# Selective scan: repeated matmuls into the same PSUM place, and stand-in pieces in the first image

## The chip, the cores and the metric

One core of one Trainium2 chip. The metric is the device time of the whole program in microseconds. The kernel before took 27451.21 us, the median of three runs (27438.02 to 27468.17). A difference is told against that kernel, run on the same chip.

## The reference

The input is eight images of 64 x 64 positions with 96 channels, in float32. Four layers follow one another, each as `x = x + layer(group_norm(x))`:

- Layers 0 and 2 are selective scans over four orders of the positions (rows, columns, and both backwards). With 192 inner channels, 16 states for each and `L = 4096` positions, the core of it is

```python
def step(h, inp):
    ut, dt, bt, ct = inp
    dA = jnp.exp(dt[..., None] * A4)
    dBu = (dt * ut)[..., None] * bt[:, :, None, :]
    h = h * dA + dBu
    y = jnp.einsum('bkdn,bkn->bkd', h, ct)
    return (h, y)
```

  around which stand a projection in, a 3 x 3 convolution per channel, a norm, a gate and a projection out.
- Layer 1 is a scan in chunks with one decay per head, made of matmuls.
- Layer 3 doubles the resolution by a low-pass filter along both axes (matmuls with fixed 64 x 128 matrices), applies `h @ W1.T`, a quadratic polynomial and `h @ W2.T`, and filters down again.

## The kernel before

The images are worked one after the other. Layers 0 to 2 of an image run in order; layer 3 of an image, called the slow layer here, is cut into small pieces that run *beside* the two selective scans of the next image (`slow_layer`, lines 433 to 627; `Beside`, 629 to 688). Layer 3 of the last image runs by itself at the end (`spectral_layer`).

`selective_scan` (lines 690 to 1034) is what the change touches. It goes through 32 steps: for each of four orders k, eight chunks of 512 positions. A step has six units n of 32 channels with 4 of the 16 states on 128 partitions, four groups of states side by side, so that a tile is 128 x 2048. For a unit:

- PE spreads `du` (32 channels) over 128 partitions into the PSUM tile `pu` by one matmul with a 0/1 matrix of 32 rows (`spread`, L835).
- DVE multiplies `pu` by `b` (`with_b`, L841); for two units of six POOL does it, from another copy `du2`.
- ACT makes the decays `da` in PSUM (L856), and DVE scans, two groups at a time (`scan`, L871).
- ACT copies the last state (L887), then POOL multiplies `h` by `c` in place (L892).
- PE sums `h` over the states, for three units at once, in `total_y`: one matmul that adds the direct term (L899), then twelve with 128 rows and 32 columns (L909). ACT copies the result out (L1008, L1016).

Beside that, `prepare` works ahead for the step after next: two projections on PE (L742, L752) that ACT copies out (L747, L756), softplus, and DMAs that copy `b`, `c`, `dx` and `du` to all partitions. For k = 1 and 3 the image is read by columns, through a view of 64 x 8 elements at a stride (`view`, L421).

All the order is written by hand (`tc.manual_schedule`, lines 977 to 1032): every engine takes its instructions in the order in which this loop writes them. On PE a step reads: spread of unit 1, `total_y` of the step before, spread of unit 3, up to three pieces, spread of unit 4, `total_y`, one piece, L742, sometimes a fifth piece, spread of the next step's unit 0, L752. `pu` has one PSUM buffer, under the tag `misc`, which pieces four and five share; the pieces before it, `pv` and `py` share one under the tag `py`. So a spread waits until DVE has read the `pu` before it, and a piece until ACT has copied out what stood in the buffer.

A piece is a tuple: a load, an ACT preparation, the PE part, the ACT copy of its result, a store, and how far ahead to load. `Beside.begin` runs the PE part (`op[2](ps)`), `Beside.end` the copy (`op[3](ps)`). There are 139 entries for the first scan of an image and 137 for the third layer's scan; `quota` gives a step four of them, now and then five. In the column pieces (`cols`, seven for each of 32 columns): one that filters along the height (L499), three hidden layers (L516, squared by ACT at L523), two mixes (L532, L536; copied out at L547) and one that filters down (L555). The first image has no slow layer beside it, and its lists are empty.

Of the kernel before, what the change touches and what calls it, by code (L numbers as in the profile page):

```python
# [53 lines left out]
K_TF = K_GRP + 96  # L54
# [13 lines left out]
def tile_vision_stack(  # L68
# [19 lines left out]
    nc = tc.nc  # L88
# [4 lines left out]
    def resident(name, src, shape):  # L93
        t = wp.tile(shape, F32, name=name)
        nc.sync.dma_start(t, src)
        return t

    cst = resident("cst", consts[:, :K_TF], [128, K_TF])
# [9 lines left out]
    sel = cst[:DM, K_SEL:K_RED]  # L108
    red = cst[:, K_RED:K_ID]
    ident = cst[:, K_ID : K_ID + 128]  # L110
# [38 lines left out]
    with (  # L149
# [6 lines left out]
        for i, (dtw, dtx, w) in enumerate(((dt0, dx0, w0), (dt2, dx2, w2))):  # L156
# [12 lines left out]
            for k in range(K):  # L169
                pw = pp.tile([DM, 2, 192], F32, name="pw", bufs=2)  # L170
                for hf in range(2):
# [4 lines left out]
                        start=True,  # L176
                        stop=True,
# [255 lines left out]
    def slow_layer(prev):  # L433
# [3 lines left out]
        pool = [None]  # L437
# [8 lines left out]
        def rows(j):  # L446

            def load():
                if j % 2 == 0:
                    live["xs", j] = xs = wide("sx")[:DM]  # L450
                    nc.sync.dma_start(xs, xd[:, j * 256 : j * 256 + 512])

            def norm():
                if j % 2 == 0:
                    live["xn"] = xn = wide("sn")[:DM]
                    nc.scalar.activation(
                        xn, live["xs", j], AF.Identity, scale=sb[:, 0:1], bias=sb[:, 1:2]
                    )

            def turn(ps):  # L460
                pt = ps[:64, : 4 * DM].rearrange("p (i c) -> p i c", i=4)
                for i in range(4):
                    at = (j % 2) * 256 + 64 * i
                    nc.tensor.transpose(pt[:, i, :], live["xn"][:, at : at + 64], ident[:DM, :DM])

            def turned(ps):
                live["xt"] = xt = narrow("st", "g")
                nc.scalar.copy(xt[:64].rearrange("p i c -> p (i c)"), ps[:64, : 4 * DM])

            def across(ps):  # L470
                nc.tensor.matmul(
                    ps[:, : 4 * DM],
                    up,
                    live["xt"][:64].rearrange("p i c -> p (i c)"),
                    start=True,
                    stop=True,
                )

            def crossed(ps):
                live["x1"] = x1 = wide("sw")[:, : 4 * DM]  # L480
                nc.scalar.copy(x1, ps[:, : 4 * DM])

            def store():
                nc.sync.dma_start(
                    x1d[4 * j : 4 * j + 4].rearrange("h w c -> w h c"),
                    live["x1"].rearrange("p (h c) -> p h c", h=4),
                )

            return [(load, norm, turn, turned, None, 4), (None, None, across, crossed, store, 0)]

        def cols(n):

            def load():
                live["c1"] = c1 = narrow("sc", "x1")[:64]
                nc.sync.dma_start(c1, x1d[:, 4 * n : 4 * n + 4])

            def down_h(ps):
                for i in range(4):
                    nc.tensor.matmul(  # L499
                        ps[:DM, i * 128 : i * 128 + 128],  # L500
                        live["c1"][:, i, :],
                        up,
                        start=True,
                        stop=True,
                    )

            def fine(ps):
                live["x2"] = x2 = wide("s2")[:DM]
                nc.scalar.copy(x2, ps[:DM])
                live["f"] = []  # L510

            ops = [(load, None, down_h, fine, None, 4 if n else 0)]
            for m in range(3):

                def hidden(ps, m=m):
                    nc.tensor.matmul(  # L516
                        ps, w3as[:, m * 128 : (m + 1) * 128], live["x2"], start=True, stop=True
                    )

                def square(ps, m=m):  # L520
                    f = wide("sf")
                    live["f"].append(f)
                    nc.scalar.activation(f, ps, AF.Square, bias=b1q[:, m : m + 1])  # L523

                ops.append((None, None, hidden, square, None, 0))
            for p in range(2):

                def mix(ps, p=p):
                    for i in range(2):
                        at = (2 * p + i) * 128  # L530
                        po = ps[:, i * DM : i * DM + DM]
                        nc.tensor.matmul(  # L532
                            po, live["x2"][:, at : at + 128], w12, start=True, stop=False
                        )
                        for m in range(3):
                            nc.tensor.matmul(  # L536
                                po,
                                live["f"][m][:, at : at + 128],
                                w2q[:, m, :],
                                start=False,  # L540
                                stop=(m == 2),
                            )

                def mixed(ps, p=p):
                    if p == 0:
                        live["g"] = narrow("sg", "g")
                    nc.scalar.copy(  # L547
                        live["g"][:, 2 * p : 2 * p + 2, :].rearrange("p i c -> p (i c)"),
                        ps[:, : 2 * DM],
                    )  # L550

                ops.append((None, None, mix, mixed, None, 0))

            def lower(ps):
                nc.tensor.matmul(  # L555
                    ps[:64, : 4 * DM],
                    down,
                    live["g"].rearrange("p i c -> p (i c)"),
                    start=True,
                    stop=True,  # L560
                )

            def lowered(ps):
                nc.scalar.copy(
                    live["g"][:64].rearrange("p i c -> p (i c)"), ps[:64, : 4 * DM]
                )

            def store():
                nc.sync.dma_start(
                    g2d[4 * n : 4 * n + 4].rearrange("w h c -> h w c"), live["g"][:64]  # L570
                )

            ops.append((None, None, lower, lowered, store, 0))
            return ops

        def ends(j):
# [39 lines left out]
                    live["res"].rearrange("p (h c) -> p h c", h=4),  # L616
                )

            return [(load, shift, last, done, store, 1 if j else 0)]

        def flat(parts):
            return [op for part in parts for op in part]
# [2 lines left out]
        first = flat(rows(j) for j in range(16)) + gap + flat(cols(n) for n in range(SPLIT))  # L625
        second = flat(cols(n) for n in range(SPLIT, 32)) + gap + flat(ends(j) for j in range(16))
        return pool, (first, second)

    class Beside:

# [29 lines left out]
        def begin(self, pool, tag):  # L660
            if self.at >= len(self.ops):
                return
            op = self.ops[self.at]
            if op:
                ps = pool.tile([128, LC], F32, name="ps", tag=tag)
                op[2](ps)
                self.flush()
                self.open = (op, ps)
            else:
                self.flush()  # L670
                self.open = (None, None)

        def end(self):
            if not self.open:
                return
            op, ps = self.open
            self.open = None
            if op:
                op[3](ps)
                self.waiting = op[4]  # L680
            self.at += 1
            if self.loaded <= self.at < len(self.ops):
                self.flush()
                while self.loaded <= self.at:
                    self.load(self.loaded)
            self.prepare(self.at)
            self.ahead(self.at)


    def selective_scan(w, wdt, a, d, u, y, beside):  # L690
# [23 lines left out]
        with (  # L714
# [11 lines left out]
            pool, ops = beside  # L726
# [100 lines left out]
                nc.scalar.copy(places(db, NSG, int(k >= 2)), src)  # L827
                made[i]["db", n] = db

            def spread(t):  # L830

                m, n = made[t // units], t % units
                rows = slice(32 * (n % 3), 32 * (n % 3) + 32)
                m["pu"] = pu = pmp.tile([128, LC], F32, name="pu", tag="misc")
                nc.tensor.matmul(pu, sel[rows, :], m["du"][rows, n // 3, :], start=True, stop=True)  # L835

            def with_b(t):

# [125 lines left out]
            with tc.tile_pool(name="p_da", bufs=1, space=PSUM) as pap:  # L964
# [4 lines left out]
                states = {}  # L969
                for t in range(3):  # L970
                    enter(t)
                spread(0)
                decays(0, 0)
                decays(0, 1)
                with_b(0)
# [1 line left out]
                for t in range(total + 2):  # L977
                    n, i = t % units, t // units
# [4 lines left out]
                    elif n == 5 and quota > 4:  # L983
                        other.begin(pmp, "misc")
                    if n in (0, 3, 5) and ahead:
                        spread(t + 1)
                    elif n == 1 and t + 2 < total:
                        spread(t + 2)
                    if n == 0 and i > 0:
                        sums = total_y(i - 1, 1)  # L990
                    elif n == 3:
# [573 lines left out]
    prev = None  # L1565
    for b in range(batch):
        xd = xp.tile([DM, L], F32, name="xd")
        sb3 = sb3s[b % 2]
        pool, ops = slow_layer(prev) if prev else ([None], ((), ()))
        layers = (  # L1570
            (w0s, w0, lambda u, y: selective_scan(w0s, wdts[0], a0s, dsum[0], u, y, (pool, ops[0]))),
            (w1s, w1, lambda u, y: chunked_scan(w1s, w1, dsum[1], u, y)),
# [47 lines left out]
        prev = (xd, sb3, dst)  # L1620
# [151 lines left out]
```

## Time and profile before

| | |
|---|---|
| profiled execution | 27478.66 us |
| its span, first to last instruction | 27476.7 us |
| mean granted TensorE clock | 0.763 |
| PE busy | 23020.0 us, 91061 matmul instructions |
| DVE busy | 24006.6 us |
| POOL busy | 21792.7 us |
| ACT busy | 16531.6 us |
| DVE scans L871 | 6144 of 2282 ns |
| POOL products L892 | 3072 of 4174 ns |
| spreads L835 | 4096 instructions (two for each float32 matmul) of 904 ns |
| scans of the first image, first to last L871 | 1185.0 and 1184.6 us |
| the 14 later ones | 1223.1 to 1241.1 us |

A group in the profile reads: line, engine, operation, out<-in with its shapes, how often; then busy time, mean ns of one, and the idle time of the engine just before, with what ended it. In a line of a timeline the start and the duration stand first. A float32 matmul stands as two MATMUL instructions. A busy PE is not PE at its peak, since the granted clock changes the duration of the same instruction; PEclk shows it, as a share of full speed.

### The profile page before, as it was taken

What the parts mean: (1) busy time and instruction counts of PE and PEld (TensorE: products, weight loads), DVE (VectorE), ACT (ScalarE), POOL (GpSimd) and SP (SyncE); (2) the same over time, 40 slices, a digit from 0 to 9 for tenths busy, and PEclk for the clock granted to TensorE, in tenths of its full rate; (3) what the DMA queues carried; (4) which work ended last, traced back from release to release, by engine and by line L of the source; (5) the groups of instructions that cost most, each with busy time, mean ns of one, the idle gap of its engine ahead of it and who ended that gap; (6) DMA issues with size and microseconds to landing.
All of it is one profiled execution on the core that took longest, in us unless ns stands there. A gap on an engine that the chain in (4) does not pass through costs nothing. (4 is left out here: it accounts for less than half of the span.)

```text
span 27476.7 us, 283336 instructions
## 1 busy us (share of the span) xinstructions
PE 23020.0 (84%) x91061; PEld 8527.1 (31%) x91061; DVE 24006.6 (87%) x17105; ACT 16531.6 (60%) x29953; POOL 21792.7 (79%) x8360
## 2 busy tenths in 40 slices
PE   7787788888888888888888888888888888888888
PEld 2141222422224222242223422234222342223424
DVE  8979898798988989889898898988989889898896
ACT  5646565565655656556565565655656556565564
POOL 8949798597976979769797697976979769796694
PEclk7787777877778777787777877778777787777878
DMA  4415454154531545325453254532545325453252
GB/s 120 119 33 126 111 131 104 43 129 115 134 99 48 129 115 134 93 54 129 115 130 89 57 129 116 130 86 61 128 117 132 80 68 127 117 131 75 71 129 67
DMA packets 1681706, 2831.73 MB, mean 103 GB/s; under 512 B 434984, under 2 KB 478280, under 8 KB 1675616
## 3 DMA queue, kind: packets, MB, share of 16 engines
q1 hardware_dynamic: 1663584, 2807.32, 41.8%
q8 instruction: 730, 11.96, 0.2%
q10 hardware_dynamic: 16640, 6.29, 0.1%
q14 instruction: 752, 6.16, 0.1%
HBM read 2385.11 MB, written 427.49 MB: 102 GB/s over the span
## 5 line engine op out<-in xcount | busy, mean ns | idle before, releaser
L871 DVE TENSOR_TENSOR_SCAN h<-da,db 128x1026 f32<-128x1026 f32 x6144 | 13775.7, 2282 | 751.3 <-ACT da L856 446.0
L892 POOL TENSOR_TENSOR h<-h,c 128x2048 f32<-128x2048 f32 x3072 | 12774.4, 4174 | 1129.8 <-ACT state L887 571.0
L909 PE MATMUL py<-h,cst 128*32 128x512 f32 x24576 | 5331.0, 788 | 105.4 <-POOL h L892 105.0
L841 DVE TENSOR_TENSOR db<-pu,b 128x2048 f32<-128x2048 f32 x2048 | 4652.1, 2272 | 625.5 <-PE pu L835 616.7
L856 ACT ACTIVATE da<-dx,a2s 128x512 f32<-128x512 f32 x6144 | 4239.2, 690 | 1536.9 <-DVE h L871 1390.5
L856 ACT ACTIVATE da<-dx,a0s 128x512 f32<-128x512 f32 x6144 | 4239.5, 690 | 1527.6 <-DVE h L871 1379.6
L841 POOL TENSOR_TENSOR db<-du,b 128x2048 f32<-128x2048 f32 x1024 | 4649.7, 4541 | 569.6 <-ACT db L827 569.6
L835 PE MATMUL pu<-du,cst 32*128 32x512 f32 x4096 | 3328.7, 904 | 1203.6 <-DVE db L841 1070.1
L909 PEld LDWEIGHTS py<-h,cst 128*32 128x32 f32 x24576 | 1207.3, 140 | 4828.1 <-issue 4366.2
L742 PE MATMUL pv<-u,wk 96*96 96x512 f32 x2048 | 1502.1, 864 | 556.6 <-ACT y L1016 444.4
L835 PEld LDWEIGHTS pu<-du,cst 32*128 32x128 f32 x4096 | 811.4, 246 | 3234.7 <-DVE db L841 1612.8
L752 PE MATMUL pv<-u,wk 96*128 96x512 f32 x2048 | 1590.7, 911 | 54.3 <-ACT raw L747 53.3
L899 PE MATMUL py<-y,cst 96*96 96x512 f32 x1536 | 1506.6, 1078 | 6.4 <-ACT state L887 6.4
L516 PE MATMUL ps<-s,w3as 96*128 96x512 f32 x1344 | 998.0, 833 | 544.8 <-ACT sf L523 188.1
L1285 ACT ACTIVATE sg<-sg 128x768 f32<-128x768 f32 x1024 | 820.5, 801 | 838.1 <-PE sg L1269 838.1
L887 ACT COPY state<-h 128x4 f32<-128x4 f32 x3072 | 591.9, 193 | 864.4 <-DVE h L871 862.5
L1239 POOL TENSOR_TENSOR ce<-ec,cr 112x512 f32<-112x512 f32 x256 | 529.0, 2066 | 717.3 <-ACT ec L1237 699.0
L1317 DVE TENSOR_TENSOR wt<-wt,cbm 128x768 f32<-128x768 f32 x1024 | 991.4, 1003 | 117.0 <-ACT wt L1286 116.3
L536 PE MATMUL ps<-w3bs,sf 128*128 128x96 f32 x5376 | 1043.9, 349 | 0.0
L1216 POOL TENSOR_TENSOR rr<-lr,cc 128x768 f32<-128x768 f32 x256 | 376.5, 1471 | 758.5 <-ACT lr L1214 753.4
L319 POOL TENSOR_SCALAR xn<-xs,sb 96x512 f32<-96x512 f32 x192 | 203.3, 1060 | 972.3 <-PE pz L324 486.2
L536 PEld LDWEIGHTS ps<-w3bs,sf 128*128 128x128 f32 x5376 | 964.6, 263 | 0.0
(241 smaller groups left out, 30528.9 us busy)
## 6 DMA issues: line engine op xcount, KB each, us to landing
dx<-dd SPq DMA_DIRECT2D x4096, 192.0 KB
b<-bcd SPq DMA_DIRECT2D x2048, 256.0 KB
c<-bcd SPq DMA_DIRECT2D x2048, 256.0 KB
du<-dud SPq DMA_DIRECT2D x2048, 128.0 KB
dd<-raw SPq DMA_DIRECT2D x1024, 192.0 KB
dud<-du SPq DMA_DIRECT2D x512, 128.0 KB
xd<-xs SPq DMA_DIRECT2D x256, 192.0 KB
cr<-bcd SPq DMA_DIRECT2D x1536, 32.0 KB
```

The lines of the kernel that those rows point to most:

```text
L516: nc.tensor.matmul(ps, w3as[:, m * 128 : (m + 1) * 128], live["x2"], start=True, stop=True)
L536: nc.tensor.matmul(po, live["f"][m][:, at : at + 128], w2q[:, m, :], start=False, stop=(m == 2),)
L742: nc.tensor.matmul(pv[:DM], weights[k][:, hi, 128:], uv[hi], start=(hi == 0), stop=(hi == 1))
L752: nc.tensor.matmul(pv, weights[k][:, hi, :128], uv[hi], start=(hi == 0), stop=(hi == 1))
L835: nc.tensor.matmul(pu, sel[rows, :], m["du"][rows, n // 3, :], start=True, stop=True)
L841: (nc.gpsimd if pool else nc.vector).tensor_mul(groups(m["db", n]), (m["du2"][:, n // 3, :] if pool else m["pu"]) .unsqueeze(1) .to_broadc ...
L856: nc.scalar.activation(dst[:, g, :LC], made[i]["dx"][n // 3][:, n % 3, :], AF.Exp, scale=av4[:, k, n, gs : gs + 1],)
L871: nc.vector.tensor_tensor_scan(made[i]["h", n][:, at][:, way], das[p][:, rev : 2 * SEG + rev][:, way], made[i]["db", n][:, at][:, way], 0. ...
L892: nc.gpsimd.tensor_mul(h, h, made[i]["c"])
L899: nc.tensor.matmul(py, skip[:, hf, :] if k == 0 else ident[:DM, :DM], view((u if k == 0 else y)[:, hf, :], wh, c * LC, LC), start=True, st ...
L909: nc.tensor.matmul(py[32 * q : 32 * q + 32, :], red, hs[q][:, g, :], start=False, stop=(g == NSG - 1),)
L1317: nc.vector.tensor_mul(it["wt"], it["wt"], m["cbm"][:, j : j + 1, :].to_broadcast([128, RK, Q]),)
```

## The change

The number of times that PE makes the same result is written into the loop. Each copy starts anew at the same place (`start=True`), so the result does not change.

- `spread` gets a count. The spreads of units 0 and 1 are made twice, that of unit 3 three times, that of unit 4 once; the very first once.
- Every piece gets a seventh entry, the count: two for all but the mixes, which keep one. `Beside.begin` runs the PE part that often.
- In the first image, where the lists were empty, 138 stand-in pieces are put beside each of the two scans: a matmul of the identity (128 rows) with 384 columns of constants, made twice, whose result nobody reads or copies.

Nothing changes on DVE, POOL or the DMA queues; ACT's work is the same.

```diff
-            return [(load, norm, turn, turned, None, 4), (None, None, across, crossed, store, 0)]
+            return [(load, norm, turn, turned, None, 4, 2), (None, None, across, crossed, store, 0, 2)]
...
-            ops = [(load, None, down_h, fine, None, 4 if n else 0)]
+            ops = [(load, None, down_h, fine, None, 4 if n else 0, 2)]
...
-                ops.append((None, None, hidden, square, None, 0))
+                ops.append((None, None, hidden, square, None, 0, 2))
...
-                ops.append((None, None, mix, mixed, None, 0))
+                ops.append((None, None, mix, mixed, None, 0, 1))
...
-            ops.append((None, None, lower, lowered, store, 0))
+            ops.append((None, None, lower, lowered, store, 0, 2))
...
-            return [(load, shift, last, done, store, 1 if j else 0)]
+            return [(load, shift, last, done, store, 1 if j else 0, 2)]
...
+    def busy(ps):
+        nc.tensor.matmul(ps[:, :K_TF], ident, cst, start=True, stop=True)
+
+    idle = [(None, None, busy, None, None, 0, 2)] * 138
...
                 ps = pool.tile([128, LC], F32, name="ps", tag=tag)
-                op[2](ps)
+                for _ in range(op[6]):
+                    op[2](ps)
...
-                op[3](ps)
+                if op[3]:
+                    op[3](ps)
...
-            def spread(t):
+            def spread(t, times):
...
-                nc.tensor.matmul(pu, sel[rows, :], m["du"][rows, n // 3, :], start=True, stop=True)
+                for _ in range(times):
+                    nc.tensor.matmul(
+                        pu, sel[rows, :], m["du"][rows, n // 3, :], start=True, stop=True
+                    )
...
-                        spread(t + 1)
+                        spread(t + 1, 1 if n == 3 else 2)
                     elif n == 1 and t + 2 < total:
-                        spread(t + 2)
+                        spread(t + 2, 3)
...
-        pool, ops = slow_layer(prev) if prev else ([None], ((), ()))
+        pool, ops = slow_layer(prev) if prev else ([None], (idle, idle))
```

## The prediction

> **What bounds the kernel.** I read the page first, then who waited for whom on DVE, then two steps of a scan in order of time, then the granted clock in stretches of 1 us. A "step" is one 512-column chunk, six units; a scan has 32 steps, and 16 scans make 512 steps.
>
> ```profile
> PE 23020.0 (84%) x91061; PEld 8527.1 (31%) x91061; DVE 24006.6 (87%) x17105; ACT 16531.6 (60%) x29953; POOL 21792.7 (79%) x8360
> L841 DVE TENSOR_TENSOR db<-pu,b 128x2048 f32<-128x2048 f32 x2048 | 4652.1, 2272 | 625.5 <-PE pu L835 616.7
> L835 PE MATMUL pu<-du,cst 32*128 32x512 f32 x4096 | 3328.7, 904 | 1203.6 <-DVE db L841 1070.1
> ```
>
> No engine is full over the span, but in a scan DVE and POOL nearly are. A step has 12 scans of 2.24 us and four products of 2.27 us on DVE: 36.0 us. POOL has six products of 4.17, two of 4.54 and du: about 36.5. So a step can hardly be under 36.25 us (a step's length is the distance between the same instruction in two steps: L835 at 234.56 and 270.81 in the trace). PE waits for DVE 1070 us at L835, so it has room. The question is when its results come. DVE's waits, largest first:
>
> ```profile
> DVE db L841 <- PE pu L835: 616.7, 388, 5.5
> DVE h L871 <- ACT da L856: 446.0, 606, 8.4
> ```
>
> Nearly all of the 617 us stands at one place. Sorted by place in the step, 538 us is the product of the *next step's unit 0*. It is unlike in two kinds of steps. In scans k = 1 and 3 the image is read turned (64x8 elements at a stride), in k = 0 and 2 plainly. A turned step of the first image:
>
> ```profile
> 600.52 3.65 PE L742 MATMUL pv<-u,wk 96*96 96x512 f32 x4 [1.80 <-ACT state L887]
> 604.11 2.01 PE L835 MATMUL pu<-du,cst 32*128 32x512 f32 x2
> 606.15 2.29 DVE L841 TENSOR_TENSOR db<-pu,b 128x2048 f32<-128x2048 f32 x1 [1.55 <-PE pu L835]
> 609.76 2.07 PE L835 MATMUL pu<-du,cst 32*128 32x512 f32 x2
> 612.95 2.27 DVE L841 TENSOR_TENSOR db<-pu,b 128x2048 f32<-128x2048 f32 x1
> ```
>
> L742 takes 3.65 us, the spread behind it 2 us, and DVE loses 1.55. This step takes 38.07 us (609.76 to 647.83). A plain step:
>
> ```profile
> 264.03 1.96 PE L742 MATMUL pv<-u,wk 96*96 96x512 f32 x4 [2.27 <-ACT y L1016]
> 265.92 1.12 PE L835 MATMUL pu<-du,cst 32*128 32x512 f32 x2
> 268.49 2.27 DVE L841 TENSOR_TENSOR db<-pu,b 128x2048 f32<-128x2048 f32 x1
> ```
>
> Here L742 takes half as long, the spread too, and it is ready 1.45 us before DVE takes it. Why does the spread cost 2.07 us in one and 1.12 in the other? The clock (the last three columns are PEclk, DMA share, GB/s):
>
> ```profile
> 602.00:603.00 1.00, 1.00 (x2) 0.18 (x1) 1.00 (x2) 0.00 (x0) 1.00 (x2) 1.00 0.47 160
> 604.00:605.00 1.00, 1.00 (x2) 0.44 (x2) 0.60 (x1) 0.74 (x2) 1.00 (x1) 0.60 0.65 193
> 606.00:607.00 1.00, 1.00 (x2) 0.50 (x2) 0.85 (x1) 0.97 (x5) 1.00 (x2) 0.50 0.00 0
> 611.00:612.00 1.00, 1.00 (x2) 0.24 (x2) 1.00 (x1) 0.97 (x2) 1.00 (x2) 0.50 0.26 66
> ```
>
> PE is busy in every one of these microseconds, yet the clock falls from 1 to 0.5 at 604.2 and stays there until 617.8, in the middle of L909.
>
> **What holds the clock: rule against rows.** The change keeps PE busier. The Trainium skill (TensorE: Matmul & The Clock Gate, Part 1) says that the gate watches how busy PE is in free-running windows of about 3.4 us: one busy window releases full clock, an idle one takes it away. The trace agrees on the grid (the clock changes only at multiples of 3.413 us) but not on "busy". I compared each window with the clock of the next. At half clock, windows full of L258 or L337 (96 rows, plain) mostly raise it, 0.7 of a window of L909 (128 rows) does; where spreads (32 rows) fill 0.4 to 0.6 of a window and other matmuls as much (0.4 to 0.6), none of 460 or so raised it. At full clock a window is held by about half a window of 96-row work; a spread's time counts there about 0.4 of that. Full windows of turned L742 kept the clock in 0 of 36, since it reads at half the rate (1.03 us an instruction against 0.59 for plain). So I take work as rows times columns moved, not time busy. By the page's rule the added copies hold the full clock everywhere (first rival below). By the rows they can't in a turned step: from L742 (3.65 us) over the spread, turned L752 and the next spread, some ten us hold nothing that counts as half, so the clock falls there as it does now.
>
> **The change, part by part.** *One more copy* of a spread is two instructions, 1.71 us at half clock, 0.86 at full (their spacing in L909: 0.86 and 0.43). DVE waits for the last copy. Per step four spreads become eight: 6.9 us of PE at half clock, 3.4 at full. PE is busy 26 us of a first-image step, 32.7 of 38.6 later, so it fits as a sum; what counts is each place.
>
> 1. Turned steps, unit 0 (twice): the copy is straight on DVE's path. Now 24 of 32 such steps in the first image and 183 of 224 later wait there. 30 and 41% of these spreads begin at full clock, fewer would end so, and I take the copy at full in a quarter: 0.25 x 0.86 + 0.75 x 1.71 = 1.50 us. 207 x 1.50 = 310, and half of it for the other 49 steps: 37. **+347.**
> 2. Turned steps, unit 1 (twice): it comes behind L752 at half clock; ready at 611.83, taken at 612.95, 1.12 spare. 1.71 - 1.12 = 0.59 in 256 steps. **+151.**
> 3. Plain steps, unit 0: 1.45 us spare hides a copy at full clock (0.86); if that cover is gone it costs 0.9 to 1.7. The 112 steps of 256 that wait already pay 1.28, the middle of both clocks. **+143.** Unit 1 has 2.7 spare: nothing.
> 4. Unit 3 (three times): 7 us between it and DVE's use cover it, as does a half-clock copy. Unit 4 stays single: nothing. But pieces queue behind the triple.
> 5. Pieces beside (first layer 139, third 137; 4 a step and a fifth in 20 steps an image): a doubled L516 takes 1.98 us at full clock, 2.07 single at half, so where the clock is held a copy is free. The fifth stands between L742 and the spread: 5 of 7 column pieces are doubled, 0.93 us on average in 140 steps, 130, of which plain steps cover some. **+100.** The other pieces: ACT copies each out in order, and POOL's product waits behind ACT (POOL h on ACT state, 571 us now). Bounds: nothing, if they run at full clock (59 to 70% begin so now), and 1.7 us a step and more if not. I take nothing, as most begin at full.
> 6. Stand-ins in the first image: 128 rows x 384, two copies, 1.28 us at full clock, 2.56 at half; no copy-out, no DMA. Three fit into the 9.7 us that PE waits before unit 4's spread. They hold the clock there but not up to L742. Between -57 (64 steps from 37.14 to 36.25) and +60: I take nothing.
> 7. Relief: where the clock now holds longer, totals L909 and the unmultiplied mixes (L536) come sooner. DVE waits 80 us after unit 3 and 150 before unit 5's second scan in later images; half of it. **-115.**
>
> Sum: 347 + 151 + 143 + 100 - 115 = +626 us. The profiled execution took 27478.7 us (span 27476.7); with it 28105, and the median of runs stands 0.1% below: **28080**.
>
> **Rivals.** *The clock holds* (faster). If busy time is what counts, or if pieces and triples bridge the gaps of the plain steps, all copies run at 0.86. Turned steps keep their 1.5 us (L742 stays 3.65, doubled spread 1.98 against 2.07: 256 x 1.5 = 384 of the 617 us stays), and of the 446 us on ACT 0.34 a step stays, as in the shortest steps. 233 + 270 at most, some 400 likely: 27050. For it: the stand-ins and L516 count fully. Against: 604.2. It decides at L742: full clock over that spread in most steps means this. Chance 0.16. *Half clock takes the pieces too* (slower still): after the triple spread (2.6 us that count 0.4) PE idles until y is copied, the clock falls, three doubled pieces cost 1.2 us more each at half clock, ACT and POOL wait behind them: about 2 us more in 448 steps, 28950. For it: totals that run sooner leave longer gaps. Against: L909 now ends so late at half clock that the next window is safe. 0.21. *It all falls into PE's idle time* (no difference), since PE waits for DVE 1070 us: 27450 within 55; against it speaks the 1.55 us above. 0.06. The likeliest: 0.57, 27700 to 28450.
>
> Range: down into the first rival, up to the centre of the second, 27300 to 28950; left out is about 0.11 below and 0.08 above. Faster by over 0.2% (what a measurement can tell from no change) 0.17, within 0.05, slower 0.78.
>
> **What would show it.** Turned steps: unit 0's spread at 3.7 us rather than 2.07, DVE's wait there near 3 us, the wait for PE over all from 617 to some 1200 us; unit 1 in turned steps waiting about 0.6; steps of the first image near 40 where they were 38.07, plain ones at 36.3 to 37. I am wrong if PEclk in the scans rises from 0.72 to 0.85 or more while DVE's wait for PE shrinks, or if ACT's waits for pieces (L547 674 us, L523) double.

## The result, and the profile after

The changed kernel takes 28576.85 us (median of 4 runs, 28567.69 to 28611.54) against 27458.74 before on the same chips: ratio 1.0411, 95% interval [1.0393, 1.0429], +1118 us. The forecast was +626 us, 28080, in a range of 27300 to 28950.

Lines move by 7 to 10: L835 is now L843, L841 is L851, L742 and L752 are L749 and L759, L871 is L881, L909 is L919. From the page of the changed kernel, its totals and the groups that answer to those shown:

```profile
PE 25737.0 (90%) x101605; PEld 9970.3 (35%) x101605; DVE 24063.2 (84%) x17105; ACT 16541.4 (58%) x29953; POOL 21772.0 (76%) x8360
L851 DVE TENSOR_TENSOR db<-pu,b 128x2048 f32<-128x2048 f32 x2048 | 4662.8, 2277 | 1343.6 <-PE pu L843 1322.2
L843 PE MATMUL pu<-du,cst 32*128 32x512 f32 x8160 | 5165.0, 761 | 443.3 <-DVE db L851 324.7
```

DVE, ACT and POOL do the same work in nearly the same time; PE has 10544 instructions more. One spread instruction became faster (761 ns against 904), because the mean clock rose from 0.763 to 0.816. Yet DVE waits for spreads 1322 us where it was 617. DVE's waits in the changed kernel:

```profile
DVE db L851 <- PE pu L843: 1322.2, 791, 7.5
DVE h L881 <- ACT da L866: 649.6, 558, 9.0
```

The second line, 446 before, says that ACT too is late with the decays. Two of the things that it waits for (ACT's waits, changed kernel; L763 copies out L759, L523 a piece):

```profile
ACT raw L763 <- PE pv L759: 1219.3, 385, 5.1
ACT sf L523 <- PE ps L516: 954.3, 630, 2.8
```

The same two waits in the kernel before:

```profile
ACT raw L756 <- PE pv L752: 781.5, 380, 3.9
ACT sf L523 <- PE ps L516: 189.3, 308, 1.1
```

A turned step of the first image, in order of time:

```profile
552.88 3.65 PE L749 MATMUL pv<-u,wk 96*96 96x512 f32 x4 [3.20 <-ACT state L897]
556.46 3.77 PE L843 MATMUL pu<-du,cst 32*128 32x512 f32 x4
560.16 3.78 PE L759 MATMUL pv<-u,wk 96*128 96x512 f32 x4
560.27 2.29 DVE L851 TENSOR_TENSOR db<-pu,b 128x2048 f32<-128x2048 f32 x1 [3.32 <-PE pu L843]
563.88 3.78 PE L843 MATMUL pu<-du,cst 32*128 32x512 f32 x4
567.69 2.29 DVE L851 TENSOR_TENSOR db<-pu,b 128x2048 f32<-128x2048 f32 x1 [0.55 <-PE pu L843]
```

Unit 0's doubled spread takes 3.77 us where one took 2.01, and DVE waits 3.32 us where it was 1.55. Unit 1's comes 0.55 late, where it had been early. The clock over this stretch (third column from the end):

```profile
552.00:553.00 1.00, 0.12 (x1) 0.12 (x2) 1.00 (x2) 1.00 (x4) 1.00 (x1) 1.00 0.42 94
553.00:554.00 1.00, 1.00 (x2) 0.34 (x3) 1.00 (x1) 0.97 (x2) 1.00 (x1) 0.67 0.03 8
555.00:556.00 1.00, 1.00 (x2) 0.00 (x0) 1.00 (x1) 0.00 (x0) 1.00 (x2) 0.50 0.32 107
559.00:560.00 1.00, 1.00 (x2) 0.00 (x0) 0.00 (x0) 0.97 (x2) 1.00 (x2) 0.50 0.00 0
```

It falls within L749, at 553.4, and stays at half through both doubled spreads, until 573.8, though PE is busy all the time in each of the last three stretches shown. By kind of step, from the distance between scans: in the first image plain steps went from 36.60 to 39.34 us and turned ones from 37.71 to 40.64; later from 37.89 to 39.59 and from 39.49 to 41.85. The share of time at full clock went up in all four, later from 0.46 to 0.60 and from 0.40 to 0.57. So the clock did rise, and the steps became longer.

### The profile page after: what moved, and what is told of

Read it like the earlier page. It is cut to its first block, busy times and chain, and to the rows that moved or that the text cites. A ratio compares the mean times of both kernels' runs of the same rounds, so it can differ in the third digit from the quotient of the medians.

```text
span 28609.8 us, 304424 instructions
## 1 busy us (share of the span) xinstructions
PE 25737.0 (90%) x101605; PEld 9970.3 (35%) x101605; DVE 24063.2 (84%) x17105; ACT 16541.4 (58%) x29953; POOL 21772.0 (76%) x8360
## 5 line engine op out<-in xcount | busy, mean ns | idle before, releaser
L881 DVE TENSOR_TENSOR_SCAN h<-da,db 128x1026 f32<-128x1026 f32 x6144 | 13782.7, 2283 | 1062.1 <-ACT da L866 649.6
L851 DVE TENSOR_TENSOR db<-pu,b 128x2048 f32<-128x2048 f32 x2048 | 4662.8, 2277 | 1343.6 <-PE pu L843 1322.2
L843 PE MATMUL pu<-du,cst 32*128 32x512 f32 x8160 | 5165.0, 761 | 443.3 <-DVE db L851 324.7
L919 PE MATMUL py<-h,cst 128*32 128x512 f32 x24576 | 4972.4, 738 | 169.4 <-POOL h L902 168.6
L851 POOL TENSOR_TENSOR db<-du,b 128x2048 f32<-128x2048 f32 x1024 | 4646.2, 4537 | 569.2 <-ACT db L834 569.2
L843 PEld LDWEIGHTS pu<-du,cst 32*128 32x128 f32 x8160 | 1652.0, 224 | 3680.9 <-issue 2749.4
L919 PEld LDWEIGHTS py<-h,cst 128*32 128x32 f32 x24576 | 1149.1, 132 | 4479.1 <-issue 3613.6
L749 PE MATMUL pv<-u,wk 96*96 96x512 f32 x2048 | 1496.7, 861 | 421.7 <-ACT y L1026 291.7
L516 PE MATMUL ps<-s,w3as 96*128 96x512 f32 x2688 | 1605.9, 727 | 245.1 <-ACT sf L523 163.2
L759 PE MATMUL pv<-u,wk 96*128 96x512 f32 x2048 | 1610.3, 921 | 52.0 <-ACT raw L754 52.0
L909 PE MATMUL py<-y,cst 96*96 96x512 f32 x1536 | 1385.1, 993 | 1.6 <-ACT state L897 1.5
L523 ACT ACTIVATE sf<-ps,w3bs 128x512 f32<-128x512 f32 x672 | 461.2, 686 | 954.3 <-PE ps L516 954.3
L763 ACT COPY raw<-pv 128x512 f32<-128x512 f32 x512 | 298.7, 583 | 1220.6 <-PE pv L759 1219.3
L516 PEld LDWEIGHTS ps<-s,w3as 96*128 96x128 f32 x2688 | 531.7, 218 | 1184.5 <-issue 505.8
```

Of the source, the lines that this page charges most:

```text
L516: nc.tensor.matmul(ps, w3as[:, m * 128 : (m + 1) * 128], live["x2"], start=True, stop=True)
L749: nc.tensor.matmul(pv[:DM], weights[k][:, hi, 128:], uv[hi], start=(hi == 0), stop=(hi == 1))
L759: nc.tensor.matmul(pv, weights[k][:, hi, :128], uv[hi], start=(hi == 0), stop=(hi == 1))
L851: (nc.gpsimd if pool else nc.vector).tensor_mul(groups(m["db", n]), (m["du2"][:, n // 3, :] if pool else m["pu"]) .unsqueeze(1) .to_broadc ...
L881: nc.vector.tensor_tensor_scan(made[i]["h", n][:, at][:, way], das[p][:, rev : 2 * SEG + rev][:, way], made[i]["db", n][:, at][:, way], 0. ...
L909: nc.tensor.matmul(py, skip[:, hf, :] if k == 0 else ident[:DM, :DM], view((u if k == 0 else y)[:, hf, :], wh, c * LC, LC), start=True, st ...
```

## The experiments

Theory 1 is that a copy costs where another engine waits for it, and that 32-row copies don't hold the clock. Theory 2 is that the doubled pieces, through ACT, are the main cause. Theory 3 is that PE simply has too much work.

### One part at a time

**Spreads alone**: pieces once, no stand-ins.

```diff
-                for _ in range(op[6]):
+                for _ in range(1):
...
-        pool, ops = slow_layer(prev) if prev else ([None], (idle, idle))
+        pool, ops = slow_layer(prev) if prev else ([None], ((), ()))
```

> The changed kernel with every piece made once and no stand-ins: only the spreads are repeated (2, 2, 3, 1). Theory 1 (a copy costs where DVE waits for it, at half clock; 32-row copies do not hold the clock): the spreads carry more than half of the +1118 us, 28050 to 28250 us; unit 0's wait of DVE (after n5) rises from 538 to 900 or more. Theory 2 (the doubled pieces hold ACT, and POOL and DVE behind it): the spreads alone cost under 300 us, below 27760. Theory 3 (PE has too much work, wherever it stands): the cost goes by added instructions, 4064 of 10544, so 430 us, 27890.

28410.75 us, ratio 1.0343 [1.0326, 1.0361], +934: more than theory 1 gave, far above the others. DVE's wait after unit 5 is 1056 us (538 before). The run's clock, and DVE's wait for spreads over all:

```profile
core 0: 28393.9 us, clock 0.761
```

```profile
DVE db L851 <- PE pu L843: 1363.7, 784, 7.1
```

4064 more PE instructions and PE busy for 89% of the span where it was 84%, and yet the clock stays at 0.761 (0.763 before). The 32-row copies did not raise it.

**Pieces and stand-ins alone**: every spread once.

```diff
-                        spread(t + 1, 1 if n == 3 else 2)
+                        spread(t + 1, 1)
...
-                        spread(t + 2, 3)
+                        spread(t + 2, 1)
```

> The changed kernel with every spread made once: pieces doubled as in the change, stand-ins in the first image. Theory 1: a doubled piece at full clock takes as long as a single one at half clock, so 100 to 450 us above before, 27560 to 27900. Theory 2: 700 us or more, above 28160. Theory 3: 6480 of 10544 added instructions, about 690 us, 28150. If the pieces (96 and 128 rows) hold the clock and nothing else is late, it is below 27400.

28010.43 us, ratio 1.0201 [1.0184, 1.0219], +533, clock 0.795. Above theory 1's range and below the others': the pieces cost more than I had allowed, but they are not the larger part.

**Unit 0 once**, the rest of the change kept.

```diff
-                        spread(t + 1, 1 if n == 3 else 2)
+                        spread(t + 1, 2 if n == 0 else 1)
```

> The changed kernel, but unit 0's spread is made once (unit 1 twice, unit 3 three times, pieces doubled). Theory 1: DVE's wait after unit 5 goes back from 972 us to about 540, and unit 1 is on time in turned steps again (-100): 500 us below the changed kernel, 28000 to 28150. Theory 2: within 150 us of the changed kernel, 28430 to 28580. Theory 3: 1024 fewer instructions of 10544, -110 us, 28470.

28248.31 us, ratio to before 1.0281 [1.0266, 1.0297], +771. That is 347 less than the +1118 of the whole change, so a little above theory 1's range and far from the other two. DVE's wait after unit 5 came back to 510 us as theory 1 says, but not all of that reached the end: the waits after unit 3 and at unit 5's second scan stayed, 292 and 320 us in later images (80 and 150 before). Nor was unit 1 on time again: it still waits 141 us (158 in the changed kernel).

**Stand-ins alone**, on the kernel before (the count is used for pieces without a copy-out only, and every spread is made once).

```diff
-                for _ in range(op[6]):
+                for _ in range(op[6] if op[3] is None else 1):
```

> The kernel before with the stand-ins of the first image alone (138 beside each of two scans, each made twice); nothing else is repeated. Only 64 of 512 steps change. Theory 1: 128-row work in PE's idle time, no copy-out: between -57 and +60 us, 27400 to 27520. Theory 3: 1104 more instructions, +117 us, 27575.

27532.48 us, ratio 1.0022 [1.0015, 1.003], +55: the upper end of theory 1's range. First-image steps are 0.7 to 0.8 us longer, although their time at full clock went from 0.44 to 0.63 (plain) and from 0.38 to 0.54 (turned). The trace has most of it at unit 0: DVE's wait after unit 5 went from 10 to 35 us over the 32 plain steps and from 38 to 58 over the turned ones. In the plain ones fewer of unit 0's spreads begin at full clock, 0.38 where it was 0.56: the clock is higher elsewhere and lower where DVE waits. In the turned ones that share rose (0.30 to 0.40), so the cause there stays open.

### Do rows count, or busy time?

Spreads alone as above, but the added copies have 128 rows:

```diff
-                for _ in range(times):
-                    nc.tensor.matmul(
-                        pu, sel[rows, :], m["du"][rows, n // 3, :], start=True, stop=True
-                    )
+                for _ in range(times - 1):
+                    nc.tensor.matmul(pu[:, :K_TF], ident, cst, start=True, stop=True)
+                    nc.tensor.matmul(pu[:, K_TF:], ident, cst[:, :128], start=True, stop=True)
+                nc.tensor.matmul(pu, sel[rows, :], m["du"][rows, n // 3, :], start=True, stop=True)
```

> As the run with repeated spreads alone (pieces once, no stand-ins), but each added copy of a spread is a matmul of the identity with constants, 128 rows instead of 32 and as many columns (384 + 128), ahead of the one spread. As many columns pass through PE at the same places. If rows count for the clock: granted clock above 0.80 (it stayed at 0.761 with 32 rows), and the cost falls from +934 to +350 to +750 us, since the copies on DVE's path stay. If busy time alone counts: clock 0.76 and 28350 to 28470 us as before.

28027.51 us, ratio 1.0195 [1.0179, 1.0211], +546 against +934. Its clock:

```profile
core 0: 28035.6 us, clock 0.810
```

As many columns at the same places, four times the rows: 0.810 against 0.761, and 388 us less. Busy time alone would have it the other way round, since PE is busy for 24283 us here and for 25167 with 32 rows. One rival stays: the added copies also move constants in place of `du`, and no run changes the data alone. The copies still cost 546 us, since they stay ahead of what DVE waits for.

**Unit 3 alone**, with 32 and with 128 rows (the second has the diff above as well):

```diff
-                        spread(t + 1, 1 if n == 3 else 2)
+                        spread(t + 1, 1)
```

> The kernel before with unit 3's spread made three times, nothing else. The prediction's step 4 has nothing for it, since DVE uses it 7 us later: 27450 to 27600 us. If the pieces that queue behind it matter (they start some 1.7 us later): +150 to +400 us. Clock unchanged by 32 rows at 0.76.

> The kernel before with two 128-row copies (constants) ahead of unit 3's spread, where nobody waits for it at once. If rows count for the clock, full clock lasts into the pieces behind it: less than the run with 32-row copies at this place by 50 to 300 us, perhaps below the kernel before (27250 to 27500), clock 0.78 or more. If busy time counts: the same as with 32 rows.

27547.56 us, 1.0024 [1.0015, 1.0032], +66; and 27526.4 us, 1.0015 [1.0009, 1.0022], +45. The two intervals overlap. With 128 rows the clock is 0.779 (0.765 with 32), and the hoped-for gain did not come. Its trace shows where it went: DVE waits less at unit 5's second scan (120 us, 150 before) but more after unit 5 (565 against 491, later images). I argue, without a run for it, that a total that ends sooner leaves PE a longer gap ahead of L742.

### Each spread alone

```diff
-                        spread(t + 1, 1 if n == 3 else 2)
+                        spread(t + 1, 2 if n == 5 else 1)
...
-                        spread(t + 2, 3)
+                        spread(t + 2, 1)
```

> The kernel before with unit 0's spread made twice, nothing else. The prediction's steps 1 and 3: 347 + 143 = +490 us, 27850 to 28100, with DVE's wait after unit 5 from 538 to some 1030 us. The rival, too much work on PE wherever it stands: 1024 of 4064 added spread instructions, a quarter of +934, 27710.

28044.36 us, 1.0203 [1.0189, 1.0217], +563, clock 0.759. DVE's waits in this run, the line for spreads:

```profile
DVE db L851 <- PE pu L843: 1148.3, 424, 7.1
```

617 + 531 = 1148: nearly the whole +563 is this wait, and all of it stands after unit 5 (538 before, 1078 here). The rival's +229 is out. So is work "wherever it stands": these are 992 more instructions, unit 3's copies were 2048 and cost 66.

The traces also sort unit 0's waits more sharply than the prediction did. L742 works for the step after next, so what counts beside a spread is how L742 reads there, not whether the step itself is turned. Sorted by that, unit 0 waits before the change at all 32 places of the first image with a turned read and at 216 of 224 later, and with a plain read at none of 28 and 61 of 196. Its copy adds 375 us at the turned reads (step 1: 347) and 167 at the plain ones (step 3: 143).

For unit 1 the count is `2 if n == 0 else 1`:

> The kernel before with unit 1's spread made twice, nothing else. The prediction's step 2: +151 us, 27600 to 27680. What is left of +934 after unit 0 (+563) and unit 3 (+66): +305 us, 27750 to 27820; if that is right, the copy also holds up the total behind it and the copy of y.

27617.17 us, 1.0056 [1.0041, 1.0071], +156. In later images 108 us of new waiting stands ahead of unit 1's product in turned steps and 34 in plain ones, where there was none before. The three alone make 563 + 156 + 66 = 785; together they make 934. So 149 us come only from their being together; the rest of +934 that unit 1 was to explain (305) is not unit 1's.

### Which pieces?

On the kernel before, with doubled pieces four and five only (`tag == "misc"`), or one to three only (`tag == "py"`); no stand-ins.

```diff
-                for _ in range(op[6]):
+                for _ in range(op[6] if tag == "misc" else 1):
```

> The kernel before with only the fourth and fifth piece of a step doubled (those that stand around L742; mixes once, no stand-ins). The prediction's step 5 has +100 for the fifth. If the place just ahead of L742 and unit 0's spread is what costs: +200 to +350 us of the 478 that the doubled pieces cost without the stand-ins.

27673.31 us, 1.0076 [1.0061, 1.0091], +212. DVE's wait at unit 5's second scan goes from 150 to 273 us: ACT is late with its decays, as it has the piece to copy out first. In 261 of these us the last thing that ACT waited for ahead of the decays was a piece.

> The kernel before with only the first three pieces of a step doubled (those behind unit 3's spread; mixes once, no stand-ins). The prediction has nothing for them (full clock doubled as long as half clock single): 27430 to 27530. If ACT's copies out hold the decays, unit 4's spread comes late (DVE waits after unit 3, 80 us now, above 200): +150 to +350 us.

27938.17 us, 1.0166 [1.0149, 1.0183], +477, clock 0.779. My "nothing" is out. DVE's waits in this run:

```profile
DVE db L851 <- PE pu L843: 855.4, 451, 5.5
DVE h L881 <- ACT da L866: 591.7, 719, 9.2
```

The first line is 239 us more than before; after unit 3 alone 80 us became 297. The pieces stand ahead of unit 4's spread on PE. The two halves together cost less than their sum: all pieces with the stand-ins cost 533, so 478 without the stand-ins' 55, against 477 + 212 = 689.

### What makes unit 0 late in turned steps

On the kernel before; the turned steps' projections read the image plainly. That leaves the turned order out of these projections (so delta, b and c of those steps belong to other positions).

```diff
-                uv = [view(u[:, hf, :], wh, at, LC) for hf in range(2)]
+                uv = [view(u[:, hf, :], False, at, LC) for hf in range(2)]
```

> The kernel before, with L742 and L752 reading the image plainly in the turned steps too (k = 1 and 3); so the projections of those steps are made from the positions in the wrong order, and all else is as before. If the reading at a stride is what makes unit 0 late there (3.65 us against 1.96, and the clock falls during it): turned steps become as long as plain ones, 1.1 us less in 32 and 1.6 less in 224, 27000 to 27150 us, DVE's wait after unit 5 in turned steps from 401 us to 100 to 200, clock above 0.77. If the turned steps are longer for another reason (the views of u and y elsewhere, the copies of y): 27300 or more.

27147.95 us, ratio 0.9881 [0.9864, 0.9897], -324. L742 in the kernel before, then this run's lines for the spread's reader and for L742:

```profile
L742 PE MATMUL pv<-u,wk 96*96 96x512 f32 x2048 | 1502.1, 864 | 556.6 <-ACT y L1016 444.4
```

```profile
L841 DVE TENSOR_TENSOR db<-pu,b 128x2048 f32<-128x2048 f32 x2048 | 4644.5, 2268 | 242.9 <-PE pu L835 234.0
L742 PE MATMUL pv<-u,wk 96*96 96x512 f32 x2048 | 1082.5, 654 | 437.3 <-ACT y L1016 318.6
```

L742 goes from 864 to 654 ns, the wait for spreads from 617 to 234 us, that after unit 5 in turned steps from 401 to 83. Turned steps are 36.82 us in the first image (37.71) and 38.35 later (39.49). So the strided reading of L742 and L752 is the larger part of what sets them apart, not all of it: later they are still 0.7 us longer than plain ones, and what that is stays open.

## Why the prediction was right, point by point

The direction held, and so did the mechanism of steps 1 to 3: a copy costs its length where DVE waits for it, at the clock of that place. Two sizes were off, one each way. The measured time lies above what was called the likeliest case (27700 to 28450) and within the range. That the total was off by no more is in part luck, since pieces priced far too low and a relief priced far too low have opposite signs. Each part alone, against the kernel before measured beside it:

| step | forecast | measured alone |
|---|---|---|
| 1 and 3, unit 0 twice | 347 + 143 = 490 | 563 |
| 2, unit 1 twice | 151 | 156 |
| 4, unit 3 three times | 0 | 66 |
| 5, pieces doubled | 100 | 477 early, 212 late, 478 together |
| 6, stand-ins | 0 | 55 |
| 7, relief | -115 | see below |
| all | 626 | 1118 |

- **Steps 1 to 3 are right in size and place.** One more 32-row copy at half clock costs 1.71 us, and the changed step shows it: 3.77 against 2.01, and 0.55 late at unit 1 where 0.59 was worked out. In the first image the clock falls during 20 of the 32 L749 with a turned read, and in the other 12 it was at half already.
- **Step 4** named the pieces behind the triple but priced them at nothing: 66.
- **Step 5 is the term that was mis-sized.** It said that a doubled L516 at full clock (1.98) is as long as a single one at half (2.07), "so where the clock is held a copy is free". That is the wrong pair. The pieces L516 before and after, 672 of them in both:

```profile
L516 PE MATMUL ps<-s,w3as 96*128 96x512 f32 x1344 | 998.0, 833 | 544.8 <-ACT sf L523 188.1
L516 PE MATMUL ps<-s,w3as 96*128 96x512 f32 x2688 | 1605.9, 727 | 245.1 <-ACT sf L523 163.2
```

In the trace before 66% of the single L516 pieces begin at full clock and take 1.12 us; the mean of all is 998.0 / 672 = 1.49. In the changed kernel it is 1605.9 / 672 = 2.39, with 80% at full clock. So the copy costs about 0.9 us though the clock is better, up to three times a step ahead of unit 4's spread, and ACT's copy-out, with decays behind it, comes later by as much. The very share that I cited for "most begin at full" (59 to 70%) was the reason why nothing could be gained. 477 us early and 212 late, 478 together, where I had 100.
- **Step 7, relief, is larger than forecast.** The parts alone add to 563 + 156 + 66 + 477 + 212 + 55 = 1529, all together to 1118. The 411 us less come from how the parts act together: the three spreads cost 149 more together than alone, the two halves of the pieces 211 less, and spreads beside pieces and stand-ins 349 less (934 + 533 against 1118). Unit 0's copy shows how. Alone it costs 563, added to all the others 347. Its wait after unit 5 then grows by some 455 us where it grew by 540 alone, and two other waits become shorter: after unit 3 from 292 to 207, at unit 5's second scan from 320 to 249. So here more of the saving is waits that overlap than copies that run faster. For the rest of the 411 no run parts the two; the clock of 0.816 (0.759 to 0.779 in the single parts) speaks for some of the latter.
- **Rule against rows.** Rows sort the traces better than busy time, as the prediction had it. I weighed PE's busy time in each stretch of the 3.413 us grid by rows / 128 (half of that for turned reads at full clock) and asked for the one bound that best tells the clock of the next stretch. In the trace before it is right in 94.5% of the stretches at half clock and 97.1% of those at full clock, in the changed kernel in 94.6 and 97.3%. By busy time alone it is 91.5% at full clock (87.6% in the changed kernel), and at half clock no better than saying that nothing changes (72%). Two readings were too strong. Of 24 stretches at full clock that a turned L742 fills to 0.95 or more, 6 were followed by full clock again (13 of 37 in the changed kernel), where the prediction has 0 of 36. And L909 with little else beside it raised the clock in 61 of 61 stretches that it filled to 0.8 to 0.9, but in none of 8 at 0.7 to 0.8.
- **The rivals.** "The clock holds" is out: the clock rose, yet unit 0 is late by more. "No difference" is out. "Half clock takes the pieces too" has the place right (pieces ahead of unit 4, ACT behind) and the cause wrong: most pieces run at full clock.
- **What should show it.** The wait for spreads was to reach some 1200 us: 1322. First-image turned steps near 40: 40.64. Plain ones 36.3 to 37: wrong, 39.34. Two causes are seen there: the stand-ins alone make them 0.83 us longer, and in the changed kernel only a quarter of unit 0's spreads in such steps begin at full clock, so the 1.45 us that should cover the copy don't: DVE's wait after unit 5 is 83 us in these 32 steps where it was 10. ACT's waits for pieces doubling was named as a sign of being wrong, and it came in part: L523 went from 189 to 954, L547 from 674 to 537. It belongs to step 5.

None of the kernels that compute the reference beats the kernel before. The nearest is the 128-row copies at unit 3, at 1.0015.

## What to carry to other kernels

Work that is added to hold a clock has a place like any other work: at the head of a queue that another engine waits for, it costs its own length, and the faster clock gives back less than that. Before doubling an instruction, ask what the single one takes *now, at the clock it mostly gets*, not at the worst clock. And a higher mean clock says nothing of the place that matters: the stand-ins raised it in the first image and made unit 0 later. If a matmul is late, look also at how it reads its operand: plain reads in two projections were worth 324 us here.

## What the runs showed of the hardware

- The granted clock went with the number of rows at work rather than with busy time. Added copies with 32 rows left it at 0.761 (PE busy 25167 us), as many columns with 128 rows took it to 0.810 (24283 us). Busy time weighed by rows told the clock of the next 3.413 us right in 94.5% (at half clock) and 97.1% (at full) of the stretches of the trace before.
- A float32 matmul whose moving operand is read at a stride (64 x 8 elements) takes 1.03 us an instruction at full clock against 0.59 for a plain one, and about the same at half clock (1.04 and 1.06). So it gains almost nothing from full clock. In the kernel before the clock fell from full to half during 30 of the 32 turned L742 of the first image; later it stayed at full through 77 of 224.
